# The order of the engines' queues in an AdaLN block with gated delta-rule attention: a planner in the kernel's source in place of the list scheduler's choice

## The chip, the cores and the metric

The kernel runs on one core of a Trainium2 chip. The metric is the device time of one execution in microseconds; the time before is the median of three runs. Durations and waits are read from one profiled execution, whose own time is given beside its span.

## The reference, cut to what matters

The input x is 8 sequences of 256 tokens by 256 channels, in 32-bit floats throughout. A small conditioning product gives a shift, a scale and a gate for each half of the block:

```python
h = _layernorm(x, axis=-1) * (1 + ca) + sa
x = x + ga * _L0_attn_ref(h, ...)
h = _layernorm(x, axis=-1) * (1 + cb) + sb
x = x + gb * _L0_ffn_ref(h, L0_ffn_w_gate, L0_ffn_w_up, L0_ffn_w_down)
```

The attention has 16 key heads of 128, each with two value heads. Queries, keys and values are projections followed by a causal convolution of four taps; queries and keys are normalised; a state of 128 by 128 for each value head is carried over the tokens:

```python
Sk = jnp.einsum('bhi,bhipj->bhpj', k_t, S)
dv = b_t[..., None] * (v_t - Sk)
upd = jnp.einsum('bhi,bhpj->bhipj', k_t, dv)
S = S * d_t[:, :, None, :, None] + upd
o = jnp.einsum('bhi,bhipj->bhpj', q_t, S)
```

The outputs are normalised, multiplied by silu of another projection (z), and projected back to 256 channels. The feed-forward half computes silu(gate) * up over 1024 hidden values, keeps the two largest magnitudes of every four, and projects back.

## The kernel before

The recurrence is worked in chunks of 128 tokens, two per sequence, as matrices: within a chunk a triangular system is solved, and the second chunk takes over what the first leaves. The sequences go in four pairs (bp), the heads of a pair in groups of four (GH), so that there are 16 groups and 64 steps of one head for one pair. The engines are named PE (TensorE), DVE (VectorE), ACT (ScalarE), POOL (GpSimd) and SP (SyncE, which here only issues DMAs).

For each group, ahead of its use, stage_a projects the keys (ps_k, L432), convolves them (ACT at L418, then three DVE passes at L420), takes norms (L447 and L451), builds the decay matrix with one DVE scan (L551, from dbc, a DMA that spreads decays over all partitions, and diag, made on POOL at L516), and forms the triangular matrix a_t (L563), whose 32x32 diagonal blocks go to DRAM (scr). stage_b loads these blocks for the whole group (blk) and inverts them on DVE in 30 steps (L604, L610). levels, once for two heads, joins the inverses of 32 to 64 and of 64 to 128 with small matmuls of 32x32 and 64x64 (L707 to L751). For each head, prepare projects query and two values (ps_qv, L432), convolves them into cv by the same lines L418 and L420, and projects z (ps_z, L646). attend works one sequence of a head: transposed values vn (L773, L778), the products ps_kq (L785 to L789) with cross and aq (L792, L794), u, ks and o (L804 to L832), the second chunk (L847, L853), the norm rs by a power on POOL (L105) and og (L871); og is transposed (ps_gt, L887) some rounds later, and shares adds the output projection of two heads (ps_y, L901). feed_forward, for 128 tokens of a finished pair, is spread over a group of the next pair (ps_ff, L190; ps_out, L244); those of the last pair form the tail after the last head.

PSUM is eight banks, in three pools: ps_in has three (projections, norms, convolutions, ps_y), ps_inv two (ps_kk, levels, feed-forward) and ps_mix three (attend). SBUF tiles have a tag and a number of buffers; w_ff has three outside the tail and eight in it, and dbc, diag and blk have one.

What sets the order before: the source emits instructions in interleaved rounds. In each round of a head the generators in turns (the two attends, levels, prepare, shares, the late transposes) take a step, and then along() lets the background (the next group's stage_a and stage_b) and the feed (a feed-forward or the next pair's tokens) advance in proportion to the rounds done. The framework's list scheduler then orders each engine's queue, by its own model of durations, with this order as priority, and it gives tiles their buffers as it goes. It does that on the dependences and on order edges that carry no semaphore: issue_after(ins) puts what a block emits on an engine behind ins. Such edges hold the loads of weights behind the first tokens and the first decays, order PE by hand in first_group, keep the matmul work of the first two heads behind that (order[0]), and the rest of them behind the last step of the first solve (first_solved).

Of the kernel before, what the change touches and what calls it, by code (L numbers as in the profile page):

```python
# [18 lines left out]
P = 128  # L19
# [7 lines left out]
GH = 4  # L27
PE1 = P + 1


# [18 lines left out]
def adaln_block(  # L49
# [36 lines left out]
    ps_inv = ctx.enter_context(tc.tile_pool(name="ps_inv", bufs=2, space=PSUM))  # L86
    ps_mix = ctx.enter_context(tc.tile_pool(name="ps_mix", bufs=3, space=PSUM))

    def bank(pool, shape, name):
# [70 lines left out]
    def feed_forward(pool, b, n, y_all, w_bufs=3):  # L160
# [19 lines left out]
        for j in range(NG):  # L180
            hj = hid[:, j]
            for i in range(0, 4, 2):
                ps = bank(ps_inv, [P, 2, 2, P], "ps_ff")
                for a in range(2):
                    w = pool.tile([P, CC, 2, P], F32, tag="w_ff", name="w_ff", bufs=w_bufs)
                    with tc.issue_after(begun["decays"]):
                        nc.sync.dma_start(out=w, in_=w_ff[j, i // 2, a])
                    for l in range(2):
                        for k in range(CC):
                            nc.tensor.matmul(  # L190
                                ps[:, a, l, :],
                                lhsT=w[:, k, l, :],
                                rhs=h2[:, k, :],
                                start=(k == 0),
                                stop=(k == CC - 1),
                            )
                nc.scalar.activation(hj[:, i : i + 2], ps[:, 0], AF.Silu)
                nc.vector.tensor_tensor(  # L198
                    out=hj[:, i : i + 2], in0=hj[:, i : i + 2], in1=ps[:, 1], op=ALU.mult
                )  # L200
                yield
# [164 lines left out]
    with ExitStack() as scope:  # L366
# [112 lines left out]
        def stage_a(kh, bp, hp, wk, h_bp, scr):  # L479
# [16 lines left out]
            else:  # L496
# [18 lines left out]
            )  # L515
            done = nc.gpsimd.tensor_tensor(  # L516
                out=diag,
# [3 lines left out]
            )  # L521
            with tc.issue_after(done.ins):
                nc.gpsimd.tensor_tensor(out=nk, in0=n2f, in1=halves[:, : 2 * NCH], op=ALU.pow)
            yield rec
# [52 lines left out]
        def stage_b(scr, scr_x, scr_y):  # L577
# [23 lines left out]
            for j in range(1, Q - 1):  # L601
# [7 lines left out]
                )  # L609
                solved = nc.vector.tensor_tensor(  # L610
                    out=blk[:, 0:j, j + 1 :], in0=blk[:, 0:j, j + 1 :], in1=tmp, op=ALU.subtract
                )
                yield solved.ins
                if j == Q // 2:
# [312 lines left out]

        last = [None]

        def scratch_of(scratch):  # L930
# [4 lines left out]
            return scr  # L935

        order = [None]

        def first_group(filled, recs, scratch):
# [6 lines left out]
            def step(gen, n=1):  # L946
                for _ in range(n):
                    with tc.issue_after(order[0]) if order[0] else ExitStack():
                        got = next(gen, None)
                    order[0] = next(  # L950
                        i for i in reversed(nc.cur_bb.bb.instructions) if i.engine == mybir.EngineType.PE
                    )
                return got
# [18 lines left out]
            for gen in (filled, *heads):  # L972
                assert next(gen, filled) is filled
            for done in stage_b(scr, *scratch):
                last[0] = done or last[0]

        def ahead(g, recs, scratch):
# [8 lines left out]
            for hp in range(GH + 1):  # L986
# [4 lines left out]
                if hp > 0:  # L991
                    for _ in waiting.pop(0):
                        yield 3.0
            for done in stage_b(scr, *scratch):
                last[0] = done or last[0]
                yield 1.0

        def all_of(gen):
            for _ in gen:
                pass  # L1000
# [19 lines left out]
        def begin(kh, bp, h_bp, by_products=0):  # L1020
            wh = two.tile([P, WI], F32, tag="wh", name="wh")
            with tc.issue_after(begun["tokens"]) if bp == 0 and kh < GH else ExitStack():
                nc.scalar.dma_start(out=wh, in_=w_heads[kh, :, :WI])
# [5 lines left out]
        prepared = []  # L1029
        with tc.issue_after(order[0]):  # L1030
            for kh in range(2):
                prepared.append(begin(kh, 0, tokens(0), 3 - 2 * kh))


        wmod_gates = two.tile([P, CC, 2, C], F32, tag="wo", name="wmod_gates", bufs=1)
        with tc.issue_after(begun["tokens"]):
            nc.scalar.dma_start(out=wmod_ss[:, :, 2:4], in_=wmod_v[:, :, 3:5, :])
# [29 lines left out]
        og_p = wo = shared = None  # L1067
        first_solved = last[0]
        waiting = iter(())
        units = []  # L1070
        head = 0
        for g, (bp, k0) in enumerate(groups):
# [22 lines left out]
            for hp in range(GH):  # L1095
                rec = recs[hp]
                if head < 2:

                    gen, shared = prepared[head]
                    with tc.issue_after(first_solved):  # L1100
                        all_of(gen)
                if head == 0:
# [3 lines left out]
                if hp % 2 == 0:  # L1106
                    turns.append(waiting)
                    og_p = two.tile([P, 2, 2, NCH, 2, P], F32, tag="og_p", name="og_p", bufs=1)
                    wo = two.tile([P, 2, 2, C], F32, tag="wo", name="wo", bufs=1)
                    with tc.issue_after(begun["tokens"]) if g == 0 else ExitStack():  # L1110
                        nc.scalar.dma_start(
# [21 lines left out]
                while turns:  # L1133
                    with tc.issue_after(first_solved) if head == 0 else ExitStack():
                        turns = [t for t in turns if next(t, turns) is not turns]
                    along()
# [13 lines left out]
    while units:  # L1150
        units = [u for u in units if next(u, units) is not units]


# [60 lines left out]
```

## Time and profile before

| what | before |
|---|---|
| median of three runs (lowest to highest) | 2107.66 us (2104.73 to 2112.7) |
| the profiled execution's own time | 2106.59 us |
| its span, first to last instruction | 2104.6 us |
| mean granted clock of PE | 0.991 |
| instructions | 45727 |
| ps_qv, ps_z, ps_y at L432, L646, L901: busy | 365.7, 252.1, 236.3 us |
| DVE taps at L420: busy for cv and for k_t | 409.4, 139.8 us |
| read from and written to HBM | 188.38 and 29.12 MB |

The page of a profile gives for each engine the time in which an instruction of it was running (busy), its share of the span and the number of instructions. PEld is the load of weights for a matmul, which overlaps PE. A group of the page is all instructions of one line, engine and operation, with the time its engine sat idle just before them and what ended that. A table of stretches gives busy time in parts of the span. The list of waits gives, for a waiting engine and line and for what it waited for, the microseconds in total, the number of times and the longest. In the order of time, neighbours of one group are put together with their count. A 32-bit matmul shows as two instructions on PE, a transpose as one.

### The profile page before, as it was taken

What the parts mean: (1) busy time and instruction counts of PE and PEld (TensorE: products, weight loads), DVE (VectorE), ACT (ScalarE), POOL (GpSimd) and SP (SyncE); (2) the same over time, 40 slices, a digit from 0 to 9 for tenths busy, and PEclk for the clock granted to TensorE, in tenths of its full rate; (3) what the DMA queues carried; (4) which work ended last, traced back from release to release, by engine and by line L of the source; (5) the groups of instructions that cost most, each with busy time, mean ns of one, the idle gap of its engine ahead of it and who ended that gap; (6) DMA issues with size and microseconds to landing.
All of it is one profiled execution on the core that took longest, in us unless ns stands there. A gap on an engine that the chain in (4) does not pass through costs nothing. (4 is left out here: it accounts for less than half of the span.)

```text
span 2104.6 us, 45727 instructions
## 1 busy us (share of the span) xinstructions
PE 2000.5 (95%) x16684; PEld 1583.3 (75%) x16684; DVE 1666.0 (79%) x4039; ACT 1271.3 (60%) x4260; POOL 391.1 (19%) x376
## 2 busy tenths in 40 slices
PE   8999999899999999999999989999999999999998
PEld 5567777677778777777777777777777877777877
DVE  6778887878788787788878779787978869787557
ACT  3557677766656556566665655657566655656652
POOL 3121312112121211212021121211213121121110
PEclk9999999999999999999999999999999999999999
DMA  4342414333343544434444443443444343344226
GB/s 127 99 131 72 117 55 108 99 80 105 92 115 103 125 115 102 123 105 111 140 92 111 107 123 113 114 115 99 128 110 115 97 127 110 94 121 116 66 91 218
DMA packets 356257, 230.99 MB, mean 110 GB/s; under 512 B 286265, under 2 KB 297913, under 8 KB 356033
## 3 DMA queue, kind: packets, MB, share of 16 engines
q1 hardware_dynamic: 336160, 167.53, 30.7%
q10 hardware_dynamic: 19872, 60.54, 9.3%
q8 instruction: 132, 2.16, 0.4%
q14 instruction: 93, 0.75, 0.1%
HBM read 188.38 MB, written 29.12 MB: 103 GB/s over the span
## 5 line engine op out<-in xcount | busy, mean ns | idle before, releaser
L420 DVE SCALAR_TENSOR_TENSOR cv<-ps_qv,conv_sb,cv 128x510 f32<-128x510 f32 (+2 forms) x564 | 409.4, 739 | 88.1 <-ACT cv L418 84.4
L432 PE MATMUL ps_qv<-h_bp,wh 128*128 128x512 f32 x768 | 365.7, 602 | 8.4 <-DVE cv L420 7.1
L105 POOL TENSOR_TENSOR rs<-ss,minus_halves 128x4 f32<-128x4 f32 x128 | 147.9, 1163 | 942.3 <-DVE ss L858 941.8
L646 PE MATMUL ps_z<-wh,h_bp 128*128 128x256 f32 x1024 | 252.1, 387 | 17.7 <-DVE cv L420 17.2
L901 PE MATMUL ps_y<-wo,og_p 128*128 128x256 f32 x1024 | 236.3, 380 | 2.6 <-ACT gz L653 2.2
L646 PEld LDWEIGHTS ps_z<-wh,h_bp 128*128 128x128 f32 x1024 | 186.9, 193 | 49.1 <-DVE cv L420 22.4
L838 ACT ACTIVATE junk<-o 128x128 f32<-128x128 f32 x512 | 154.2, 305 | 112.1 <-DVE o L854 96.8
L432 PEld LDWEIGHTS ps_qv<-h_bp,wh 128*128 128x128 f32 x768 | 134.3, 193 | 112.7 <-issue 100.2
L901 PEld LDWEIGHTS ps_y<-wo,og_p 128*128 128x128 f32 x1024 | 188.2, 190 | 27.7 <-ACT gz L653 3.3
L604 DVE TENSOR_TENSOR tmp<-blk 128x30 f32<-128x30 f32 (+14 forms) x480 | 156.9, 327 | 56.4 <-DMA blk<-scr 48.7
L418 ACT ACTIVATE cv<-ps_qv,conv_sb 128x512 f32<-128x512 f32 x188 | 129.3, 689 | 107.5 <-PE ps_qv L432 106.8
L516 POOL TENSOR_TENSOR diag<-consts,bk 128x1032 f32<-128x1032 f32 x64 | 123.5, 1929 | 364.5 <-DVE bk L507 329.1
L420 DVE SCALAR_TENSOR_TENSOR k_t<-ps_k,conv_sb,k_t 128x510 f32<-128x510 f32 (+1 forms) x189 | 139.8, 741 | 37.6 <-ACT k_t L418 35.6
L610 DVE TENSOR_TENSOR blk<-blk,tmp 128x30 f32<-128x30 f32 (+14 forms) x480 | 156.8, 327 | 9.6
L551 DVE TENSOR_TENSOR_SCAN e<-dbc,diag 128x1032 f32<-128x1032 f32 x60 | 138.1, 2302 | 19.5 <-POOL diag L516 13.4
L871 DVE SCALAR_TENSOR_TENSOR og<-o,rs,gz 128x128 f32<-128x128 f32 x512 | 145.8, 344 | 8.4 <-POOL rs L105 7.7
L812 PE MATMUL ps_ks<-u,cross 128*128 128x128 f32 x1024 | 141.7, 280 | 7.1 <-ACT u L806 3.9
L812 PEld LDWEIGHTS ps_ks<-u,cross 128*128 128x128 f32 x1024 | 128.7, 193 | 16.6 <-issue 6.3
L190 PE MATMUL ps_ff<-h,w_ff 128*128 128x128 f32 x1024 | 132.5, 277 | 4.2 <-ACT h L149 2.3
L190 PEld LDWEIGHTS ps_ff<-h,w_ff 128*128 128x128 f32 x1024 | 124.4, 192 | 14.9 <-issue 5.9
L778 ACT ACTIVATE vn<-ps_v,nk 128x256 f32<-128x256 f32 x256 | 104.5, 486 | 51.4 <-PE ps_v L773 51.2
L826 ACT ACTIVATE o<-ps_ks,g_in 128x128 f32<-128x128 f32 x256 | 79.9, 365 | 87.2 <-DVE rr L817 78.5
(180 smaller groups left out, 4189.9 us busy)
## 6 DMA issues: line engine op xcount, KB each, us to landing
wh<-in_w_heads ACTq DMA_DIRECT2D x64, 640.0 KB, 4.5
w_ff<-in_w_ff SPq DMA_DIRECT2D x128, 256.0 KB, 3.1
dbc<-d_dram SPq DMA_DIRECT2D x60, 516.0 KB, 3.7
wo<-in_w_heads ACTq DMA_DIRECT2D x32, 512.0 KB, 3.7
w_dn<-in_w_down SPq DMA_DIRECT2D x64, 256.0 KB, 3.0
wk<-in_w_keys SPq DMA_DIRECT2D x16, 512.0 KB, 3.5
scr<-a_t SPq DMA_DIRECT2D x256, 32.0 KB, 2.1
blk<-scr SPq DMA_DIRECT2D x16, 512.0 KB, 4.5
```

The costliest lines, as they stand in the source:

```text
L105: nc.gpsimd.tensor_tensor(out=out, in0=in_, in1=minus_halves[:, :n], op=ALU.pow)
L190: nc.tensor.matmul(ps[:, a, l, :], lhsT=w[:, k, l, :], rhs=h2[:, k, :], start=(k == 0), stop=(k == CC - 1),)
L420: nc.vector.scalar_tensor_tensor(out=dst[:, :, d:], in0=ps[:, :, : T - d], scalar=taps[:, KC - 1 - d : KC - d], in1=dst[:, :, d:], op0=ALU ...
L432: nc.tensor.matmul(ps.rearrange("p b t -> p (b t)"), lhsT=w[k], rhs=h_bp[:, k, :], start=(k == 0), stop=(k == CC - 1),)
L551: nc.vector.tensor_tensor_scan(e.rearrange("p i s t -> p (i s t)"), dbc.rearrange("p i f -> p (i f)"), diag.rearrange("p s t -> p (s t)"), ...
L604: nc.vector.tensor_tensor(out=tmp, in0=blk[:, j, None, j + 1 :].to_broadcast([P, j, m]), in1=blk[:, 0:j, j, None].to_broadcast([P, j, m]), ...
L610: solved = nc.vector.tensor_tensor(out=blk[:, 0:j, j + 1 :], in0=blk[:, 0:j, j + 1 :], in1=tmp, op=ALU.subtract)
L646: nc.tensor.matmul(ps[:, n, :], lhsT=h_bp[:, k, i * T + n * P : i * T + (n + 1) * P], rhs=wh[:, k * 640 + 384 : (k + 1) * 640], start=(k = ...
L812: nc.tensor.matmul(ps_ks[:, ct, h, :], lhsT=cross[:, h, ct, :], rhs=u0[:, h, :], start=True, stop=True)
L838: nc.scalar.activation(junk, o[:, n, h, :], AF.Square, accum_out=ss[:, n, h : h + 1])
L871: nc.vector.scalar_tensor_tensor(out=og[:, n, h, :], in0=o[:, n, h, :], scalar=rs[:, 2 * n + h : 2 * n + h + 1], in1=gz[:, i, n, h, :], op ...
L901: nc.tensor.matmul(ps_y[:, n, :], lhsT=og_p[:, j // 2, i, n, j % 2, :], rhs=wo[:, j // 2, j % 2, :], start=(j == 0), stop=(j == 3),)
```

## The change

At the end of the traced program, plan_issue_order simulates all five queues and then puts one order edge, without a semaphore, between each pair of neighbours on each engine, so that the framework's scheduler has no choice left within an engine. A Step holds an instruction's reads, writes, the time after which its engine can start the next (pitch) and the time until its result is there (took), both from formulas on the number of elements. Dependences come from overlap of the tiles' elements; PSUM tiles count as a whole. A tile needs a free buffer of its tag, in the order in which the source asks for them. At each turn the engine whose earliest instruction can start first is taken; among its instructions that can start within AHEAD ns of that, the one with the lowest sum of place in the program times PACE and wait times HASTE goes next. All tail work stays behind the last instruction on every engine that uses the rec and feed pools. The holds of weight loads are passed on as pairs (behind); the other hand-made edges (POOL's power behind diag, first_group's order of PE, the first two heads behind it and behind first_solved) are dropped. The emission order of the source, all operations and all tiles stay.

```diff
+PACE = 115.0
+HASTE = 200.0
+AHEAD = 1000.0
+ENGINES = {"PE": "PE", "Activation": "ACT", "DVE": "DVE", "Pool": "POOL", "SP": "SP"}
+HANDOVER = {
+    ("PE", "ACT"): 38, ("PE", "DVE"): 38, ("ACT", "DVE"): 33, ("DVE", "ACT"): 75, ("DVE", "POOL"): 84,
+    ("ACT", "POOL"): 86, ("POOL", "DVE"): 34, ("POOL", "ACT"): 90, ("DVE", "DVE"): 38, ("ACT", "ACT"): 40,
+    ("POOL", "POOL"): 40, ("PE", "PE"): -165, ("DVE", "PE"): 55, ("ACT", "PE"): 52,
+}
...
+    def durations(self):
+        ins, e, kind = self.ins, self.engine, self.kind
+        dims = [list(d) for d in ins.outs[0].bass_ap.ap]
+        n = math.prod(d[1] for d in dims[1:])
+        psum = any(a.tensor.space == PSUM for a in self.reads + self.writes)
+        if self.is_dma:
+            return (340 if e == "ACT" else 440), 1950 + 4 * math.prod(d[1] for d in dims) // 256
+        if e == "PE":
+            self.weights = ins.ins[1].bass_ap.tensor.name
+            size = tuple(ins.tile_size) if ins.tile_size else (P, P)
+            if size[0] == size[1] < P:
+                self.square = size[0]
+                one = 10 if size[0] == Q else 33
+            elif ins.is_transpose:
+                one = 108
+            else:
+                one = 0.84 * n if n > P else 112 if n > 64 else 108
+            took = one * (1 if ins.is_transpose else 2)
+            return took, took + 165
+        if e == "DVE":
+            if kind == "InstTensorScalarPtr" and ins.is_tensor_tensor_scan:
+                took = 40 + 2.19 * n
+            elif kind == "InstStreamTranspose":
+                took = 443
+            elif kind == "InstBNStats":
+                took = 424
+            elif n < 16:
+                took = 165 if kind != "InstTensorReduce" else 678
+            elif kind == "InstTensorTensor" or not psum and kind != "InstTensorScalarPtr":
+                took = 153 + 1.03 * n
+            else:
+                took = 213 + 1.03 * n
+            return took - 82, took
+        if e == "ACT":
+            if len(ins.outs) > 1:
+                return 300, 490
+            strided = any(list(a.ap)[-1][0] not in (0, 1) for a in self.reads if len(list(a.ap)) > 2)
+            took = 210 + 0.93 * n if kind == "InstActivation" else 205 + 0.65 * n
+            if n == 4 * P and not psum:
+                took = 1107 if strided else 630
+            return took - 100, took
+        if e == "POOL":
+            if "pow" in str(getattr(ins, "op", "")):
+                took = 1020
+            elif kind == "InstMemset":
+                took = 150 + 0.8 * n
+            else:
+                took = 350 if n < 16 else 170 + 1.7 * n
+            return took - 30, took
+        return 60, 60
+def squares_between(a, b):
...
+    return 220 if b == P else 95 if a == P else 120
+def plan_issue_order(tc, held):
...
+    queue = {}
+    for name in users:
+        if tile_of[name].tag is not None:
+            queue.setdefault(tile_of[name].tag, []).append(name)
+    place = {n: i for v in queue.values() for i, n in enumerate(v)}
+    slots = {tag: tile_of[v[0]].tag_meta.bufs or 1 for tag, v in queue.items()}
...
+    def room(k):
+        when, asked = 0.0, {}
+        for n in tiles_of[k]:
+            if n not in given:
+                tag = tile_of[n].tag
+                if place[n] > nxt[tag]:
+                    return None
+                asked[tag] = asked.get(tag, 0) + 1
+        for tag, c in asked.items():
+            spare = slots[tag] - used[tag]
+            if spare < c:
+                if spare + len(freed[tag]) < c:
+                    return None
+                when = max(when, sorted(freed[tag])[c - spare - 1][0])
+        return when
...
+    for _ in range(N):
+        best = None
+        for e, some in open_now.items():
+            first, found = None, []
+            for k in some:
+                s = max(ready[k], free[e] + (squares_between(square, steps[k].square) if e == "PE" else 0))
+                if first is not None and s > first + AHEAD:
+                    continue
+                if tiles_of[k]:
+                    when = room(k)
+                    if when is None:
+                        continue
+                    s = max(s, when)
+                found.append((s, k))
+                first = s if first is None else min(first, s)
+            if first is not None and (best is None or first < best[0]):
+                best = first, e, found
+        first, e, found = best
+        begin[0], k = min(
+            ((s, k) for s, k in found if s <= first + AHEAD), key=lambda c: c[1] * PACE + HASTE * (c[0] - first)
+        )
+        s = begin[0]
+        me = steps[k]
+        open_now[e].remove(k)
+        for n in tiles_of[k]:
+            if n not in given:
+                tag = tile_of[n].tag
+                if used[tag] < slots[tag]:
+                    used[tag] += 1
+                else:
+                    freed[tag].sort()
+                    handed.append((freed[tag].pop(0)[1], k))
+                given.add(n)
+                while nxt[tag] < len(queue[tag]) and queue[tag][nxt[tag]] in given:
+                    nxt[tag] += 1
+        done[k] = s + me.took
+        free[e] = s + me.pitch
...
+        for j in me.feeds:
+            you = steps[j]
+            lag = 45 if me.is_dma else 60 if you.is_dma else HANDOVER.get((e, you.engine), 60)
+            if you.engine == "PE" != e and you.weights in me.made:
+                lag += 100
+            ready[j] = max(ready[j], done[k] + lag)
+            waits[j] -= 1
+            if not waits[j]:
+                open_now[you.engine].add(j)
+    info = mybir.DependencyInfo(mybir.DependencyClass.NoSync, mybir.DependencyReason.DATA)
+    for seq in order.values():
+        for a, b in zip(seq, seq[1:]):
+            tc.add_manual_dep(steps[b].ins, steps[a].ins.name, info, reason="issue order")
+    return max(done)
...
+    held = []
+    @contextmanager
+    def behind(ins):
+        n = len(nc.cur_bb.bb.instructions)
+        yield
+        held.extend((ins.name, i.name) for i in nc.cur_bb.bb.instructions[n:] if i.engine == ins.engine)
...
-                    with tc.issue_after(begun["decays"]):
+                    with behind(begun["decays"]):
                         nc.sync.dma_start(out=w, in_=w_ff[j, i // 2, a])
                     for l in range(2):
...
-            done = nc.gpsimd.tensor_tensor(
+            nc.gpsimd.tensor_tensor(
                 out=diag,
                 in0=identx[:, None, :].to_broadcast([P, 2 * NS, PE1]),
                 in1=bk.rearrange("p n h -> p (n h)")[:, :, None].to_broadcast([P, 2 * NS, PE1]),
                 op=ALU.mult,
             )
-            with tc.issue_after(done.ins):
-                nc.gpsimd.tensor_tensor(out=nk, in0=n2f, in1=halves[:, : 2 * NCH], op=ALU.pow)
+            nc.gpsimd.tensor_tensor(out=nk, in0=n2f, in1=halves[:, : 2 * NCH], op=ALU.pow)
             yield rec
...
-                    with tc.issue_after(order[0]) if order[0] else ExitStack():
-                        got = next(gen, None)
-                    order[0] = next(
-                        i for i in reversed(nc.cur_bb.bb.instructions) if i.engine == mybir.EngineType.PE
-                    )
+                    got = next(gen, None)
                 return got
...
         prepared = []
-        with tc.issue_after(order[0]):
-            for kh in range(2):
-                prepared.append(begin(kh, 0, tokens(0), 3 - 2 * kh))
+        for kh in range(2):
+            prepared.append(begin(kh, 0, tokens(0), 3 - 2 * kh))
...
-                    with tc.issue_after(first_solved):
-                        all_of(gen)
+                    all_of(gen)
...
-                    with tc.issue_after(first_solved) if head == 0 else ExitStack():
-                        turns = [t for t in turns if next(t, turns) is not turns]
+                    turns = [t for t in turns if next(t, turns) is not turns]
...
+    plan_issue_order(tc, held)
```

## The prediction

> **What bounds the kernel now.** I read the page's head first, then a table of stretches, then the list of who waited for whom on TensorE (PE), then the order of instructions around one long wait.
>
> The head of the page gives busy time, share of the span and instruction count of each engine:
>
> ```profile
> span 2104.6 us, 45727 instructions
> PE 2000.5 (95%) x16684; PEld 1583.3 (75%) x16684; DVE 1666.0 (79%) x4039; ACT 1271.3 (60%) x4260; POOL 391.1 (19%) x376
> ```
>
> PE is the bound and 104.1 us of the span are its gaps. That is not all that better order could win: matmul rows overlap (four of 1.88 us in all are followed by the next after 1.72), so a short wait hides under the end of the row before. I therefore also counted PE by pitch, start to start in unbroken runs of the timeline: 1.72 us for four 512-column matmuls (430 ns each), 1.73 for eight of 256 columns (216), 0.89 for eight of 128 (111), 0.87 for eight transposes (109); a block of 64 small 32x32 matmuls takes 0.86 us with the switches at its ends, one of 32 of 64x64 1.36 us. Times the counts of the groups: 1068 x 0.430 = 459; 2560 x 0.216 = 553; 5120 x 0.111 = 568; 1600 x 0.109 = 174; 192 other x 0.111 = 21; 64 blocks x 0.86 = 55; 64 x 1.36 = 87. Sum 1918 us. So 187 us of the span is not PE work: 104 in gaps and 83 under the rows.
>
> [...]
>
> Where the gaps lie (columns: stretch, its length, busy us and instructions of PE, PEld, DVE, ACT, POOL, then granted PE clock, DMA share, GB/s):
>
> ```profile
> 0.00:60.00 60.00, 49.38 (x223) 33.62 (x224) 35.67 (x93) 22.32 (x71) 19.40 (x22) 0.97 0.46 141
> 60.00:300.00 240.00, 220.30 (x1824) 166.18 (x1823) 194.04 (x482) 155.31 (x495) 47.41 (x46) 0.97 0.35 94
> 300.00:1900.00 1600.00, 1537.08 (x13110) 1219.44 (x13110) 1303.64 (x3098) 986.27 (x3345) 303.01 (x284) 0.99 0.41 109
> 1900.00:2030.00 130.00, 129.33 (x1094) 106.82 (x1093) 83.76 (x221) 82.57 (x282) 17.05 (x18) 1.00 0.28 77
> 2050.00:2104.60 54.60, 45.98 (x328) 41.94 (x328) 40.25 (x124) 13.92 (x32) 2.05 (x4) 1.00 0.68 211
> ```
>
> The reader sees 91.8% busy from 60 to 300, 96.1% from 300 to 1900, and 99.5% from 1900 to 2030. The single hundreds range from 92.7 to 99.4; 1900 to 2000 has little of the next group's preparation left (DVE 64%), but 400 to 500 (98.66) and 1400 to 1500 (98.90) have all kinds of work in them, with DVE at 81 and 83%, and nearly no gaps. So the dependences allow 98.8%; the order often does not.
>
> Who PE waited for, and one such wait (start, length, instructions):
>
> ```profile
> PE ps_z L646 <- DVE cv L420: 17.2, 15, 3.0
> PE ps_u L847 <- ACT o L826: 7.8, 10, 1.6
> PE ps_qv L432 <- DVE cv L420: 7.1, 7, 2.5
> PE ps_m L399 <- DMA wmod_ss<-in_wmod: 7.0, 1, 7.0
> ```
>
> ```profile
> 1209.70 1.88 PE L432 MATMUL ps_k<-h_bp,wk 128*128 128x512 f32 x4
> 1211.41 0.60 PE L447 MATMUL ps_n2k<-consts,k_t 128*128 128x128 f32 x4
> 1214.99 3.68 PE L646 MATMUL ps_z<-wh,h_bp 128*128 128x256 f32 x8 [2.98 <-DVE cv L420]
> 1218.47 0.43 PE L147 MATMUL ps_h<-consts,xn 128*128 128x128 f32 x2
> 1218.73 1.05 PE L812 MATMUL ps_ks<-u,cross 128*128 128x128 f32 x8
> ```
>
> No single cause dominates: the 104 us are scattered over dozens of waits. At 1214.99 PE's queue stands behind ps_z, which needs a PSUM bank that VectorE (DVE) empties with its three taps at L420; the scan at L551 (2.30 us) and two a_t products (1.28 us) stand between those taps in DVE's queue. ps_ks two lines further is other work. After the wait ps_z takes 3.68 us instead of 1.89: the profile's clock is 0.71 in 1213 to 1218, so long gaps cost twice. The mean clock of 0.991 is worth 0.009 x 2104.6 = 19 us of full-speed time, part of it in gaps.
>
> **The change part by part.** It removes no operation and adds none: 16684 matmuls and the DMAs stay. Planning happens at build time, and the order edges are of the kind without synchronisation; both cost 0 on the chip, and nothing has to hide them.
>
> *Durations.* Planner's formula against row: DVE tap of 510 columns 738 ns, row 741; scan 2300, row 2302; aq 680, row 683; og 345, row 344; ACT cv 686, row 689; ACT copy of 256 371, row 374 to 385. Worse: ACT vn and cross 448, rows 486 and 492; gz 686, row 602; POOL rs 1020, mean 1163 and longest 3033; the load of blk 4.00 us, row 4.5; that of dbc 4.01, row 3.7. Most are within 1%, the rest err by 40 to 150 ns or half a microsecond.
>
> *Steady part, 60 to 1900.* The wait above is the sort that a planner with true durations sees: at the planned start of ps_z the bank isn't free, ps_ks is startable, and a rule that takes the earliest start, with program order as a small bias (115 points a place against 200 points a ns), takes ps_ks. Bounds: nothing gained, or all of the gaps, 1840 - 1757.4 = 82.6 us, and some of the 83 under the rows besides. I take the level of the two full hundreds above, 98.8%: 1757.4 / 0.988 = 1779, **61 us less**. Nothing for what hides under the rows: the best stretches carry such waits too. The half-clock stretches go with the long gaps: between 0 and 19 us, I take 6, a third, since PE is idle in part of them and some stay.
>
> *1900 to 2030.* 99.5% busy already: 0.
>
> *Last head and tail, 2030 on.* From 2030.1 to 2042.6 the chain runs vn, cross, u, ks, o, squares, rs, og through ACT, DVE and POOL with nothing left to put beside it; from 2050 four feed-forward units alternate with DVE. PE needs 256 x 0.111 + 64 x 0.216 + 1 = 43 of those 54.6 us. Bounds: 12 gained, or 12 lost if filler was spent earlier; I take 0. The tail still may not begin before the last instruction of the pools it replaces.
>
> *Start.* The hand-made order of the first group (and the edges that kept the first two heads behind the first solve) goes. Idle in the first 60 us is 10.6, of which 7.0 is the first load, which no order shortens. Bounds: 4 gained; lost, as much again as is idle, 11. I take 0. The holds that keep ACT's and SP's weight loads behind the first tokens and decays are kept in another form: 0.
>
> *DMA queues, POOL.* SP's waits (221 us for the scan to free dbc, 202 for xb) are idle time of a queue that carries loads only. PE waited just 5.3 us for x_even and 2.2 for low_up in all. The planner reorders SP's issues at 440 ns each; the timeline shows four a_t stores in 1.80 us. Between 8 gained and 8 lost, taken as 0. The 20 table loads of ACT (1283 ns each) are not in the plan; ten more cost 13 us of an engine that is idle 40%: 0 on PE, up to 13 without that cover.
>
> **Sum.** 2104.6 - 61 - 6 = 2038 us span. The profiled execution took 2106.59, 2.0 over its span, and the median of the three runs is 2107.66, 1.1 above that: 2038 + 2 + 1 = 2041.
>
> **What is late next.** With 67 us off, DVE is 1666 / 2038 = 82% busy. Its waits (84 us for ACT's first pass of cv, 49 for blk) then lie closer to PE's.
>
> **Rivals.**
> *Near the floor.* The plan also takes the short waits under the rows: half of the 83, 41 us more, so about 2000, and 1965 at the extreme (1918 + 7 first load + 13 chain + 12 tail + some 15). For it: 15 to 165 ns waits are what exact hand-over times address. Against: two dependent matmuls often follow each other for want of a free bank.
> *No effect.* PE's gaps come from DVE order and three banks a pool, and the planner, which knows no critical path and ranks by program order, queues the scan between the taps again. DVE at 81% from 300 to 1900 speaks for it; 1400 to 1500, 98.9% with DVE at 83, speaks against. It gives 2085 to 2115. That the edges reproduce the old order is the same case.
> *Slower.* A tight static order has no slack: as PE stood behind ps_z above, each late operand holds all behind it. PE has some 1940 hand-overs (192 ps_qv, 64 ps_k, 128 each of ps_z, ps_y, ps_ks, ps_kq, and so on). 67 us / 1940 = 35 ns of unabsorbed lateness in each eats the gain; at 60 ns it is 116 us, and the kernel stands at 2108 - 67 + 116 = 2157. It decides from 35 ns on. For it: vn and cross are planned 38 and 44 ns short, blk 500. Against: gz is planned 84 ns long, and lateness is shared over streams.
> [...]
>
> **How the numbers follow.** Forecast 0.55 (2005 to 2075); near the floor 0.15; no effect 0.14; slower 0.16. 0.5% is about what a measurement of this kernel can tell from no change: 2097 to 2118. No effect is cut by 2097: 0.06 counts as faster, 0.08 as same. Faster 0.55 + 0.15 + 0.06 = 0.76, same 0.08, slower 0.16. Range: from 1975, leaving 0.04 of the floor case below, to 2115, leaving the slower case above.
>
> **What would show it.** Right: PE busy at 98% or more in most hundreds from 60 to 1900, few waits over 1.5 us, clock at 0.995 or more, unchanged tail. Wrong: PE waits spread in many short ones with the same total (slower or no effect); DVE over 90% in some hundreds with PE below 95; a longer stretch after 1900 for want of filler; PE's busy sum falling well below 1950 (the short waits went too).

## The result, and the profile after

The change made the kernel 0.9% slower: 2126.8 us, median of four runs (2124.95 to 2129.8), against 2106.5 before (median of four). The ratio is 1.0092, 95% interval 1.0068 to 1.0117. The profiled execution took 2125.81 us, with a span of 2124.1.

The head of the page after the change, in the columns shown for before:

```profile
span 2124.1 us, 45623 instructions
PE 1994.0 (94%) x16684; PEld 1581.2 (74%) x16684; DVE 1657.3 (78%) x4039; ACT 1263.1 (59%) x4260; POOL 389.9 (18%) x376
```

The work is the same, and PE's busy time is even 6.5 us less; its gaps grew from 104 to 130 us. The stretches (the tail now begins at 2054):

```profile
0.00:60.00 60.00, 49.09 (x222) 33.69 (x223) 34.77 (x95) 22.18 (x73) 19.65 (x23) 1.00 0.43 131
60.00:300.00 240.00, 215.17 (x1835) 162.15 (x1834) 196.90 (x493) 158.22 (x504) 42.34 (x44) 0.97 0.36 96
300.00:1900.00 1600.00, 1527.91 (x13096) 1214.37 (x13095) 1289.57 (x3083) 977.51 (x3352) 311.45 (x288) 0.99 0.41 109
1900.00:2030.00 130.00, 127.04 (x1085) 104.91 (x1084) 86.02 (x220) 79.58 (x265) 12.26 (x16) 1.00 0.30 77
2054.00:2124.10 70.10, 52.36 (x330) 47.53 (x328) 41.09 (x125) 14.43 (x32) 2.21 (x4) 0.87 0.54 165
```

From 60 to 1900 PE is busy 94.7% of the time (before 95.5); nothing of the hoped-for 98.8. The last row is the tail: 70 us in place of 55, PE idle for 18 of them, and a clock of 0.87.

What PE waits for (in total, times, longest):

```profile
PE ps_o L1101 <- ACT o L1102: 23.8, 12, 3.3
PE ps_ff L461 <- DMA w_ff<-in_w_ff: 16.3, 12, 2.6
PE ps_m L670 <- DVE sc_t L651: 8.3, 1, 8.3
PE ps_z L916 <- DVE cv L691: 7.8, 10, 1.4
PE ps_ff L461 <- DVE hid L469: 6.5, 1, 6.5
```

The old waits shrank as foreseen (ps_z for cv from 17.2 to 7.8 us), but the first row is new. Before, ps_o waited in this way 1.1 us in all:

```profile
PE ps_o L831 <- ACT o L832: 1.1, 3, 0.6
```

The line numbers have moved: L1101 was L831, L1102 (ACT's copy of ps_o into o) was L832, L1087 (rr) was L817, L1096 (ACT's read of ps_ks into o) was L826, L461 was L190.

A table of progress shows where the time went: the moment in each trace when the last ps_y matmul of a pair of heads begins (there are 32 pairs), and the end. The columns on the right belong to experiments below; each is one profiled execution.

| pair | before | after | PSUM readers first | rr first, start and tail free | rr first |
|---|---|---|---|---|---|
| 1 | 183.3 | 182.5 | 197.5 | 181.6 | 182.8 |
| 6 | 489.5 | 485.1 | 519.6 | 488.1 | 484.2 |
| 16 | 1107.1 | 1101.9 | 1121.0 | 1090.0 | 1077.8 |
| 24 | 1607.8 | 1607.1 | 1611.6 | 1574.1 | 1560.6 |
| 32 | 2049.5 | 2053.9 | 2045.1 | 2004.5 | 1991.3 |
| end | 2104.6 | 2124.1 | 2105.9 | 2061.5 | 2061.5 |

After the change the kernel gains 4.4 us up to pair 6, loses 8.8 from there to pair 32, and 15.1 in the tail: 19.5 in all.

The wait in its place (start, length, instructions; PE first, then DVE, then ACT):

```profile
764.62 1.05 PE L1082 MATMUL ps_ks<-u,cross 128*128 128x128 f32 x8
765.51 0.61 PE L1101 MATMUL ps_o<-u,aq 128*128 128x128 f32 x4
765.96 1.06 PE L1082 MATMUL ps_ks<-u,cross 128*128 128x128 f32 x8
...
771.48 1.13 PE L1171 MATMUL ps_y<-wo,og_p 128*128 128x256 f32 x4 [0.56 <-DVE cv L691]
775.95 1.23 PE L1101 MATMUL ps_o<-u,aq 128*128 128x128 f32 x4 [3.35 <-ACT o L1102]
```

```profile
767.83 0.73 DVE L691 SCALAR_TENSOR_TENSOR cv<-ps_qv,conv_sb,cv 128x506 f32<-128x506 f32 x1
768.48 0.38 DVE L880 TENSOR_TENSOR blk<-blk,tmp 128x228 f32<-128x228 f32 x1
768.79 0.73 DVE L691 SCALAR_TENSOR_TENSOR cv<-ps_qv,conv_sb,cv 128x510 f32<-128x510 f32 x1
...
773.81 0.41 DVE L495 SCALAR_TENSOR_TENSOR mag<-mag,c 128x256 f32<-128x256 f32 x1
774.14 0.33 DVE L880 TENSOR_TENSOR blk<-blk,tmp 128x184 f32<-128x184 f32 x1
774.40 0.33 DVE L1087 SCALAR_TENSOR_TENSOR rr<-ps_ks,g_ex,vn 128x128 f32<-128x128 f32 x1
```

```profile
775.27 0.37 ACT L1096 ACTIVATE o<-ps_ks,g_in 128x128 f32<-128x128 f32 x1 [5.89 <-DVE rr L1087]
775.54 0.36 ACT L1102 COPY o<-ps_o 128x256 f32<-128x256 f32 x1
```

Two ps_ks and one ps_o fill the three banks of ps_mix by 767. rr, which reads the first ps_ks, could run from about 766; it runs at 774.40, after taps of cv, the solver's tmp and blk and the sparsifier's mag. ACT's read of ps_ks (L1096) waits for rr, which reads the same tile, and its copy of ps_o (L1102), whose matmuls ended at 766.12, stands behind that read in ACT's queue. ACT is idle for 5.89 us, no bank comes free, and PE stands for 3.35 us. Over all 128 attends, the median time from the end of the matmuls that rr needs to its start is 1.54 us before and 5.20 after (mean 2.18 and 4.81).

That is the planner's choice, not an accident on the chip: its own plan has this wait, 3.8 us long. It ranks what can start by place in the program. This rr has place 6672 among the program's 18253 instructions; the next group's solver steps at work here, traced in earlier rounds, have places up to 6595, the taps of cv 6648 to 6662, mag 6663 to 6667. Whenever one of them is ready, it goes first.

ACT's side is a second rule of the plan. It places no instruction on a tile before the tile's first user in the program (before_me in plan_issue_order), and the first user of o is the read of ps_ks. So the copy that would have emptied ps_o's bank can't be placed ahead of a read that needs rr. In the traces the n-th copy of ps_o starts before the n-th attend's first read of ps_ks for 78 of 128 attends before, and for none after the change.

### The profile page after: what moved, and what is told of

It is laid out like the page before. It is cut to its first block, busy times and chain, and to the rows that moved or that the text cites. A ratio compares the mean times of both kernels' runs of the same rounds, so it can differ in the third digit from the quotient of the medians.

```text
span 2124.1 us, 45623 instructions
## 1 busy us (share of the span) xinstructions
PE 1994.0 (94%) x16684; PEld 1581.2 (74%) x16684; DVE 1657.3 (78%) x4039; ACT 1263.1 (59%) x4260; POOL 389.9 (18%) x376
## 4 chain that ended last, share of the span: by engine, by line
PE 54%; DVE 27%; ACT 7%; DMA 5%; issue 3%; POOL 1%; SPq 0%; ACTq 0%; DVEq 0%; POOLq 0%
PE ps_qv L703 9%; PE ps_z L916 6%; DVE cv L691 6%; PE ps_y L1171 5%; PE ps_k L703 3%; PE ps_ff L461 3%; PE ps_ks L1082 3%; DVE e L821 3%; DMA w_ff<-in_w_ff 3%; PE ps_u L1117 2%; PE ps_o L1101 2%; PE ps_gt L1157 2%; DVE blk L880 2%; DVE og L1141 2%; DVE tmp L874 2%
## 5 line engine op out<-in xcount | busy, mean ns | idle before, releaser
L691 DVE SCALAR_TENSOR_TENSOR cv<-ps_qv,conv_sb,cv 128x510 f32<-128x510 f32 (+1 forms) x564 | 412.9, 738 | 82.5 <-ACT cv L689 77.9
L376 POOL TENSOR_TENSOR rs<-ss,minus_halves 128x4 f32<-128x4 f32 x128 | 152.9, 1205 | 853.1 <-DVE ss L1128 851.5
L923 ACT ACTIVATE gz<-ps_z 128x512 f32<-128x512 f32 x128 | 77.4, 605 | 192.1 <-PE ps_z L916 192.0
L703 PEld LDWEIGHTS ps_qv<-h_bp,wh 128*128 128x128 f32 x768 | 129.2, 191 | 82.0 <-issue 77.7
L1141 DVE SCALAR_TENSOR_TENSOR og<-o,rs,gz 128x128 f32<-128x128 f32 x512 | 152.1, 344 | 16.0 <-POOL rs L376 15.4
L461 PE MATMUL ps_ff<-h,w_ff 128*128 128x128 f32 x1024 | 137.3, 286 | 26.2 <-DMA w_ff<-in_w_ff 16.3
L461 PEld LDWEIGHTS ps_ff<-h,w_ff 128*128 128x128 f32 x1024 | 127.8, 198 | 36.0 <-DMA w_ff<-in_w_ff 18.6
L1048 ACT ACTIVATE vn<-ps_v,nk 128x256 f32<-128x256 f32 x256 | 115.9, 483 | 49.2 <-PE ps_v L1043 32.3
L793 POOL TENSOR_TENSOR nk<-n2k,halves 128x4 f32<-128x4 f32 x64 | 66.4, 1038 | 428.6 <-DVE n2k L771 422.6
L1096 ACT ACTIVATE o<-ps_ks,g_in 128x128 f32<-128x128 f32 x256 | 96.1, 375 | 81.8 <-DVE rr L1087 81.4
```

The lines of the kernel that those rows point to most:

```text
L376: nc.gpsimd.tensor_tensor(out=out, in0=in_, in1=minus_halves[:, :n], op=ALU.pow)
L461: nc.tensor.matmul(ps[:, a, l, :], lhsT=w[:, k, l, :], rhs=h2[:, k, :], start=(k == 0), stop=(k == CC - 1),)
L691: nc.vector.scalar_tensor_tensor(out=dst[:, :, d:], in0=ps[:, :, : T - d], scalar=taps[:, KC - 1 - d : KC - d], in1=dst[:, :, d:], op0=ALU ...
L703: nc.tensor.matmul(ps.rearrange("p b t -> p (b t)"), lhsT=w[k], rhs=h_bp[:, k, :], start=(k == 0), stop=(k == CC - 1),)
L1141: nc.vector.scalar_tensor_tensor(out=og[:, n, h, :], in0=o[:, n, h, :], scalar=rs[:, 2 * n + h : 2 * n + h + 1], in1=gz[:, i, n, h, :], op ...
```

## The experiments

Four theories were put against each other. **P**: the planner's own ranking is at fault. **L**: the tied queues lose whatever a plan wins, since each late operand holds what is behind it. **D**: loads land later than the planner thinks. **S**, **W** and **B** came with the later kernels and are told there. The planner returns its own end of the plan, 2033 us for the change: close to the forecast's span of 2038, and 91 us short of the chip's 2124.

**PSUM readers first**

```diff
+    early = [100 if s.engine != "PE" and any(a.tensor.space == PSUM for a in s.reads) else 0 for s in steps]
-            ... key=lambda c: c[1] * PACE + HASTE * (c[0] - first)
+            ... key=lambda c: (c[1] - early[c[1]]) * PACE + HASTE * (c[0] - first)
```

> One edit to the planner's choice: an instruction of DVE or ACT that reads PSUM counts as 100 places earlier in the program. Nothing else changes. Theory P (the planner's own ranking is at fault: it goes by place in the program, so DVE leaves rr at L1087 and the like behind solver and sparsify steps, all three banks of ps_mix stay full, and PE stands): the plan's own end falls from 2033 to 1997 us, and the chip follows, 2126 - 36 = 2090 us, within 12; PE's 12 waits of ps_o at L1101 (23.8 us) go. Rival L (lateness: the queues are tied so tightly that whatever a plan wins is lost on the way; 91 us between the plan's end and the chip's span now): the lateness grows by what the plan wins, and the time stays at 2115 to 2135. Rival D (late DMAs) expects the waits for w_ff to stay at 16 us or grow, and a gain of 15 to 36 us less some of that.

Measured 2105.4 us, ratio 1.0008 (0.9981 to 1.0035): 21 us better than the change, 15 short of P and outside its margin of 12. The waits of ps_o for ACT fell to 8.0 us but did not go; those for w_ff fell to 10.9, against D. The progress table shows two parts: 30 us lost against before by pair 6, 34 won from there to pair 32. P holds for the steady part, and the start is a matter of its own. Some of the start's loss is of this execution and not of the order: the ten executions took 2094.7 to 2115.0 us at mean clocks of 0.990 to 0.982, the profiled one is at 0.982, and from 42.0 to 62.5 us it ran at half clock (0.50; last section). The trace of "both edits" below has the same planned start without that stretch, and reaches pair 6 at 508.2, 19 us behind before.

**The tail free**

```diff
     for seq in order.values():
+        seq = [k for k in seq if k not in opened]
         for a, b in zip(seq, seq[1:]):
```

Here opened holds the instructions of the tail.

> The order edges are left out for the instructions of the tail (the feed-forward of the last pair, after the last head), which the list scheduler orders again; the rest is as planned. The tail lasts 69.8 us after the change against 54.6 before. Theory P: the planner's order of the tail is at fault, the tail falls to about 55 us and the time by 15, to 2111 us. Rival L: the tail is long because PE arrives late and at half clock, its order matters little; gain of 0 to 4 us.

Measured 2108.9 us, ratio to before 1.0028 (1.0016 to 1.0041): 18 us better than the change by the medians, 13 by the ratios. In the trace the tail takes 55.2 us in place of 70.2. The tail's two long waits, as planned and then free (PE, from the timelines):

```profile
2068.12 12.77 PE L461 MATMUL ps_ff<-h,w_ff 128*128 128x128 f32 x112 [0.55 <-ACT h L420]
2087.37 13.10 PE L461 MATMUL ps_ff<-h,w_ff 128*128 128x128 f32 x96 [6.47 <-DVE hid L469]
2100.30 3.62 PE L515 MATMUL ps_out<-w_dn,hid 128*128 128x256 f32 x16
2107.96 12.31 PE L515 MATMUL ps_out<-w_dn,hid 128*128 128x256 f32 x48 [4.04 <-DVE hid L500]
```

```profile
2060.78 13.04 PE L462 MATMUL ps_ff<-h,w_ff 128*128 128x128 f32 x112 [0.60 <-ACT h L421]
2074.73 10.99 PE L462 MATMUL ps_ff<-h,w_ff 128*128 128x128 f32 x96 [0.91 <-DVE hid L470]
2086.15 5.45 PE L516 MATMUL ps_out<-w_dn,hid 128*128 128x256 f32 x24 [0.44 <-DVE hid L470]
2091.78 8.90 PE L516 MATMUL ps_out<-w_dn,hid 128*128 128x256 f32 x40 [0.18 <-DVE hid L501]
```

From 2078 to 2087 DVE does the sparsifying of all four units, as the program order has it, and only then, at 2086.91, the product at L469 that frees a bank of ps_inv for the next ps_ff; the list scheduler puts that product earlier. The plan has these waits too, 7.9 and 5.2 us long. The tail is the planner's choice.

**More time for DMAs in the plan**

```diff
-            return (340 if e == "ACT" else 440), 1950 + 4 * ...
+            return (340 if e == "ACT" else 440), 2950 + 4 * ...
```

> The planner's formula for a DMA gets 1000 ns more (2950 in place of 1950), everything else as planned. The plan's own end grows by 15 us to 2048. Rival D (loads land later than planned, w_ff by up to 3.7 us, and PE waits for them): the waits for w_ff (16.3 us) and half of the half-clock stretches behind them go, the lateness shrinks by 20 to 30 us, and the time falls by 5 to 15, to 2111 to 2121. Theory P: the plan is 15 us longer, 5 to 10 us of DMA waits go, the time stays within 8 us of 2126 or rises. Rival L: the same as P.

Measured 2125.5 us, ratio to before 1.011 (1.0087 to 1.0133): no change against the changed kernel, within P's margin and outside D's 2111 to 2121. PE's waits for w_ff halved to 8.2 us, but a wait of 6.5 us for x_even came, and ps_o's rose to 28.8. The lateness shrank by 14 us (2125.1 - 2048 = 77 in place of 91), less than D's 20 to 30, and the plan's 15 us took that back. D falls as the cause of the loss: the late loads are real (w_ff lands 2.5 to 6.7 us after its issue, where the plan has 3.0), but planning for them bought nothing, and with rr first alone (below) PE waits for w_ff just 0.5 us without it. L expected the same as P here, so this run does not part those two.

**Edges on PE alone**

```diff
-    for seq in order.values():
+    for seq in (order[e] for e in ('PE',)):
```

> Only PE's queue gets the planner's order edges; DVE, ACT, POOL and SP are ordered by the list scheduler, to which PE's order is given. Theory P: PE's order was made for a DVE that leaves rr late; the list scheduler serves PE's operands sooner, but in its own durations; the waits of ps_o at L1101 shrink; 2100 to 2126 us. Rival L: it is the tight order of DVE and ACT that holds operands back, so the time falls below before, under 2100 us. A third case, PE's fixed order and the other queues' free choice fit badly: over 2135 us.

Measured 2190.6 us, ratio to before 1.0419 (1.0383 to 1.0454): the third case, and P's 2100 to 2126 is missed too. The waits of ps_o at L1101 for ACT are gone from the list, as P expected, but PE's order fits the planned DVE and ACT, not those of the list scheduler: ps_z waits 30.6 us for cv (7.8 when all are planned), ps_w 21.0 for x_even. L, in the form that the ties on DVE and ACT do the harm, falls; they serve PE's order.

**Both edits, and then a free start**

The first two edits together; then also no edges for what the plan starts in its first 130 or 500 us, with the hand-made edges of before put back as pairs that the planner knows (shown in part, with times in ns; for 500 us the first line has 500000.0):

```diff
+        seq = [k for k in seq if starts[k] >= 130000.0]
...
+    for a, b in held:
+        tc.add_manual_dep(steps[at[b]].ins, a, info, reason="held")
...
-                    got = next(gen, None)
+                    with behind(order[0]) if order[0] else ExitStack():
+                        got = next(gen, None)
...
-                    all_of(gen)
+                    with behind(first_solved):
+                        all_of(gen)
```

> The edits of the first two experiments together: readers of PSUM on DVE and ACT count 100 places earlier, and the tail has no order edges. Where PSUM readers go first, the tail took 2105.9 - 2046 = 59 us, 5 more than the list scheduler's. Theory P: 2105 - 5 = 2100 us. Theory S (what is lost with PSUM readers first is lost in the first 500 us, at half clock, and won after): the same 2100, since the start is untouched. Rival L: no better than either, 2105 to 2109.

> As the kernel with PSUM readers first and no edges in the tail; besides, instructions that the plan starts in its first 130 us get no order edges, and the hand-made edges of the kernel before (PE's order in the first group, the first two heads behind it and behind the first solve, POOL's power behind diag) are put back, known to the planner too. The first pair of heads was done at 197.5 us with PSUM readers first against 183.3 before. Theory S: those 14 us come back, of which 10 are a half-clock stretch from 42 to 62 us, and some of the 9 lost in the next two groups stay lost: 2085 us, within 8. Rival L: the lateness moves on, 2097 to 2107.

> The same with the first 500 us of the plan left free, so that the list scheduler with its hand-made edges orders the first three to four groups. Before, the sixth pair of heads was done at 489.5 us, with PSUM readers first at 519.6; from there to the last pair it took 1560.0 us before and 1525.5 with PSUM readers first. Theory S: 489.5 + 1525.5 + 55 for the tail = 2070 us, within 10. Rival L: the gain after 500 us is a catching up of what the start fell behind (work left undone early is there to fill later gaps), so it goes when the start is faster: 2095 to 2107 us.

| kernel | median | ratio to before (interval) |
|---|---|---|
| both edits | 2102.1 | 0.9968 (0.9953 to 0.9984) |
| and the first 130 us free | 2092.0 | 0.9924 (0.9897 to 0.9951) |
| and the first 500 us free | 2079.8 | 0.9867 (0.9847 to 0.9888) |

S's figures came out within their margins, the last just (2079.8 against 2070, within 10). The traces say why only for the last: pair 6 comes at 508.2 with both edits and at 489.4 with 500 us free, and from there to pair 32 it takes 1533.4 us, against 1560.0 before. So a start of 500 us left free wins what PSUM readers first lose there, and the later gain stays; L's reading of that gain as a mere catching up falls. With 130 us free, pairs 1 and 6 come at 190.0 and 507.1, hardly other than with both edits (187.4 and 508.2): the 14 us that S expected back in pair 1 are not in these traces, and what makes that kernel 10 us faster is not shown.

**The ranking as it was, start and tail free; and rr alone**

```diff
+    early = [100 if s.engine == "DVE" and any(a.tensor.name.startswith("ps_ks") for a in s.reads) else 0 for s in steps]
```

The key that uses early is that of PSUM readers first.

> The same free start (500 us of the plan, hand-made edges put back) and free tail as the best kernel so far, but with the planner's ranking as it was: no instruction counts as earlier. The plan's own end is 2033 us, with PSUM readers first it is 2003. Theory P (the ranking costs the steady part): start as before, 489 us; from the sixth to the last pair as after the change, 1569 us; tail 55: 2113 us, within 8, so about 33 more than the best kernel. Rival B (the free start and the free tail are what helps, the ranking matters little): 2080 to 2095 us.

> The same free start and tail, and only one kind of instruction counts 100 places earlier: rr (L1087 after the change), which reads the bank of ps_ks on DVE. The plan's own end is 1983 us against 2003 with all PSUM readers first. Theory P in its narrow form (rr left behind the solver's and the sparsify's steps is what keeps the banks of ps_mix full; the other PSUM readers need no help): as good as or better than all PSUM readers first, 2055 to 2080 us, and the waits of ps_o at the matmul of the first chunk (L1101 after the change) under 5 us. Rival W (it takes all PSUM readers, the taps of cv above all): back to 2095 to 2113 us. Rival L: the plan's 20 us are lost on the way, 2080 us and no better.

> The changed kernel with one edit: rr (the DVE instruction that reads ps_ks) counts 100 places earlier. Start and tail are as the planner orders them. The plan's own end is 1979 us against 2033 for the change. Theory P in its narrow form: the steady part gains what it gained with a free start and tail, 1568.8 - 1516.4 = 52 us from the sixth to the last pair; the start (485 us) and the tail (70 us) stay: 2126 - 52 = 2074 us, within 10. Rival S (without the free start the first 500 us lose tens of us at half clock, as with all PSUM readers first, 30 us): 2095 to 2110 us. Rival L: the lateness grows by what the plan wins, 2110 us or more.

With the old ranking: 2122.9 us, 1.0079 (1.0055 to 1.0103), 2 us outside P's margin (2113, within 8) and far from B; ps_o waits 22.5 us again, so the free start and tail are not what helps. With rr alone earlier: 2066.0 us, 0.9807 (0.978 to 0.9834), and ps_o waits 3.7 us in all, under P's 5; the other PSUM readers need no help, and W falls. With rr first as the only edit to the change: **2060.8 us, 0.9769 (0.9738 to 0.9801)**, 66 us faster than the change and 13 better than P said, outside its margin of 10. S falls for this edit: the planned start is as good as before's (pair 6 at 484.2 us).

The steady part with rr first alone, and what is left of the wait (its line is L1102 there):

```profile
60.00:300.00 240.00, 217.82 (x1839) 166.32 (x1838) 197.32 (x496) 161.31 (x514) 45.60 (x46) 0.96 0.36 96
300.00:1900.00 1600.00, 1567.83 (x13602) 1254.73 (x13601) 1330.53 (x3205) 1022.05 (x3468) 300.99 (x293) 1.00 0.42 113
```

```profile
PE ps_o L1102 <- ACT o L1103: 5.7, 11, 1.2
```

From 300 to 1900 PE is now busy 98.0%, with 13602 matmul rows done in place of 13096. rr starts a median of 0.98 us after its matmuls. ACT's copy of ps_o still never goes ahead of the read of ps_ks (0 of 128), so moving rr is enough; whether letting that copy go first, with rr left as it was, would do as well was not tested.

**rr first and the tail free**

> The changed kernel with rr 100 places earlier and no order edges in the tail. With rr first alone the last pair of heads was done at 1991.3 us of the trace, and the tail took 70.2 us more; the list scheduler's tail took 55.2 us. Theory P: the two add up, 2061 - 15 = 2046 us, within 6. Rival: the two faults share a cause and don't add up, 2055 us or more.

2049.5 us, ratio to before 0.9727 (0.9696 to 0.9757), within P's margin: 11 of the 15 us, with a tail of 57.9 us in the trace. The two faults add up; this version beats both kernels. It also beats rr first with the start free as well (2066.0): with rr first, the planned start is the better one, pair 6 at 483.0 against 488.1 and pair 16 at 1076.2 against 1090.0.

## Why the prediction was wrong

*The steady part.* "A rule that takes the earliest start, with program order as a small bias, takes ps_ks": this step failed. At a PE that waits, the planner does take other work. But the wait begins on DVE, where many instructions are ready at the same moment; among equals the bias is the whole rule, and by place rr comes last. At ACT, ready work could not be taken at all, since a tile's first user must come first. Of the 61 us, none came. With rr moved, the last pair of heads is done 58 us before the kernel before, and the fault costs 62.6 us at pair 32 (2053.9 against 1991.3). That 58 is near the forecast's 61 and 6 is in part luck. PE's share from 60 to 1900 is then 97.0%, not 98.8. And the sum had no term for lateness: the plan with rr first ends at 1979, 59 us under the forecast's span of 2038, and the chip loses 82 of its own.

*The tail* was taken as 0, with 12 either way as bounds: 15 lost. The step looked at dependences and at spent filler, not at the order in which the planner would rank the four units.

*The half clock.* Six us were to come back. The clock fell from 0.991 to 0.987 instead: 0.013 x 2124.1 = 27.6 us of full-speed time lost, against 18.9. Half-clock stretches lie at the new waits: the clock is 0.50 from 774.3 to 781.1, at the end of the wait shown above and after it, and in the tail its mean is 0.87.

*Start, DMAs, table loads.* The start was taken as 0 and gained 4.4 us by pair 6. The DMA term was taken as 0 with 8 as bound: PE's waits for DMAs, the first load left out, rose from 7.8 to 19.2 us, 11 more. With rr first they are 2.6. The table loads of ACT are 20 in number before and after.

*No effect* named the right mechanism (no critical path, ranks by program order, scan or solver between what PSUM waits for), gave it 2085 to 2115 and a chance of 0.14, and ended it there: it did not see that such a ranking, with ACT's copy tied behind rr, can hold all three banks at once where the old order did not. Its evidence against, a stretch at 98.9% before, speaks of what the dependences allow, not of what this rule picks.

*Slower* gave a lateness of 35 ns for each of 1940 hand-overs as the break-even. The lateness is there: 91 us / 1940 = 47 ns, and by the rival's own sum that gives 2108 - 67 + 91 = 2132, near the 2126.8 measured. But it does not decide. It is 82 us, 42 ns each, with rr first (2061.5 - 1979.3), and that kernel is 2.3% faster than before; it is 78 with start and tail free too, and 109 with all PSUM readers first, some 10 of it the half-clock stretch. It does not grow with what the plan wins: the 54 us by which the plan with rr first is shorter arrive as 63. Matched matmul by matmul with the plan, the change's 91 us come in many small parts, some 18 of them in waits for w_ff and 19 in matmuls at half clock. What it would take to remove them stays open.

All PSUM readers first lose 30 us by pair 6 in one execution and 19 in the other, rr first none. The half-clock stretch is the most of the difference between the two; what loses the 19, nothing settles.

Three banks of ps_mix were enough: with rr first and the same three, 5.7 of the 23.8 us for which PE waited at ps_o for ACT are left. The reader that frees the bank was queued late.

## What to carry to other kernels

A planner with true durations is only as good as its tie rule: look at the engines that empty PSUM, and rank by what holds a bank, not by place in the program alone. Before such a change is priced, follow one bank from its matmul to its last reader and ask what the rule puts before that reader. Read the plan's own waits first: the 12 at ps_o and the two in the tail stood in it before the chip ran.

## What the runs showed of the hardware that was not expected

In one execution a busy PE stayed at half clock (0.50) for 20.5 us, and the same groups in the same order ran at full clock (1.00) in another. The stretch from 42 to 62.5 us, first with PSUM readers first, then with both edits (the same planned order but for the tail), then before:

```profile
42.00:62.50 20.50, 19.82 (x53) 12.54 (x54) 9.76 (x17) 0.86 (x4) 2.89 (x2) 0.50 0.37 86
```

```profile
42.00:62.50 20.50, 19.82 (x83) 11.65 (x83) 9.56 (x21) 5.23 (x13) 3.05 (x3) 1.00 0.37 86
```

```profile
42.00:62.50 20.50, 19.82 (x94) 12.11 (x93) 13.31 (x32) 5.42 (x18) 3.04 (x3) 1.00 0.46 116
```

All are busy 19.82 of 20.5 us; the first does 53 matmul rows at a clock of 0.50, the second 83 and the third 94 at 1.00. In the first two PE's queue holds the same groups in the same order here, and its eight rows of ps_cv take 6.38 us in one and 3.68 in the other. Nor did an idle stretch come before the fall: in the first, PE was busy 3.50 of the 3.50 us up to 42.0. The 20 us of nearly unbroken matmuls that followed did not bring the clock back. What decides, no run here tells; the kind and order of the work alone do not.

The time to landing of one kind of transfer spread widely: 256 KB of w_ff took 2.5 to 6.7 us after the change, with a median of 3.4, and 2.5 to 6.8 before, with a median of 3.1.
